# Third product read from PSUM in every three-term sum, blurred taps built on TensorE, and a new order at both ends of the program

## The chip, the cores and the metric

The kernel runs on one core of one Trainium2 chip. The metric is the device time of one launch in microseconds (us), as the median of several runs. Beside those runs stands one profiled execution, whose trace all the durations come from.

## The reference, cut to what matters

The input `x` is (128 samples, 64 channels, 1024 positions) in float32. Four modulated convolutions follow each other, and `x` is added to the result:

```python
TYPES = ('same', 'upsample', 'same', 'downsample')
def _layer(x, style, w, b, mw, mb, typ):
    s = style @ mw.T + mb                          # one factor per sample and input channel
    weight = SCALE * w * s[:, None, :, None]
    demod = lax.rsqrt(jnp.sum(weight * weight, axis=(2, 3)) + EPS)
    weight = weight * demod[:, :, None, None]      # one 64x64x3 filter per sample
    if typ == 'same':       out = conv_same(x, weight) + b
    elif typ == 'upsample': out = blur(conv_up(x, weight) + b, 2 * blur_k)
    else:                   out = conv_down(blur(x, blur_k), weight) + b
    return out
for i, typ in enumerate(TYPES):
    out = _layer(out, style, weights[i], biases[i], mod_w[i], mod_b[i], typ)
return x + out
```

All four layers are linear, so away from both ends of a row they are one filter of nine taps per sample (64x64 each), with the residual as an identity in the middle tap, and one constant per output channel. The three positions at each end of a row are computed separately, layer by layer.

## The kernel before, in words

**Tiling.** A pair `p` is two samples: 64 input channels of the one on the upper 64 partitions, those of the other on the lower 64. There are 64 pairs, and 32 steps `q` of two pairs each. Each matmul is 64x64 in one quadrant of the array, and four of them stand together. Everything is float32; the trace records two matmuls for each one that the program issues.

**The filter of a step.** For step `c` the nine taps are built from right to left. `scale3` (ScalarE, tiles `wd`) scales the last layer's weights; `stage1` multiplies them by layer 2's (PSUM tile `psS`, line 306) and ScalarE copies the result into `S` (line 284); `stage2` multiplies by `E` (`psR`, line 337), the seven blurred taps of layer 1, and ScalarE copies into `R`; `stage3` multiplies by layer 0's weights (`psW`, line 374, in two parts) and ScalarE copies into `Wf`. `E` is made once, at the start, by seven VectorE instructions in `blur` (line 275). `residual` adds the identity, and `combine` makes three weighted sums of the taps, `H` (lines 412 to 416, VectorE).

**The convolution of a pair.** Three output positions are computed with five products. `pre1` and `pre2` make five combinations `T` of the input's planes: VectorE makes `G` (lines 440 and 443), GpSimd (POOL) makes two of the `T` from it (447 and 448), VectorE the other three (453 and 463). `product(p, m, ...)` issues 12 matmuls for one of the five products. `convA12` issues products 1 and 2, and `convA3` product 3, into three column ranges of one PSUM tile `psA` (170 columns each; two such tiles turn, tag `u` of `ps_conv`). Products 0 and 4 are added by `convB` to the PSUM tile `Y`, which must already hold its start value. `seed` makes the start value and the middle output `y1` on VectorE: `u = -m2/3 - m1` and `v = m2/3 - m1` (lines 528 and 529), then `Y = u + m3 * (1/6, 4/6)` in one instruction for both column ranges (547) and `y1 = 2 * m3/6 + v` (548). For that, ScalarE first copies from `psA`: `-m1` (line 506, in `m1_copy`) and product 3 twice, times 1/6 and times 4/6 (519 and 520). All three copies are issued in `convA3`, behind product 3; for the last pair alone, `m1_copy` is issued in `convA12`. `output` scales `Y` and `y1` into the tile `o` (line 572, ScalarE), and `store` writes it out.

**Order.** The scheduler is off (`manual_schedule`): the order on each engine is that of the program's text, and semaphores are derived from the tiles that instructions share. One step of the main loop is: `stage2(c)`, `convB(p)`, `output(p)`, `stage3(c, 0)`, `convA12(p+2)`, `seed(p+1)`, `stage3(c, 1)`, `convA3(p+2)`, `convB(p+1)`, `output(p+1)` in both halves, `seed(p+2)`, `stage1(s)`, `scale3(s+1)`, `combine(c)`, `convA12(p+3)`, `convA3(p+3)`, with `c = q+2` and `s = q+3`. So the pairs with an even number have `stage3(c, 1)` between their products 2 and 3, and those with an odd number have nothing there. `EXTRA` and `SLOTS` put the remaining work on style factors, constants and row ends into fixed steps. `zeros_to_y` issues matmuls of zeros.

Of the kernel before, what the change touches and what calls it, by code (L numbers as in the profile page):

```python
# [50 lines left out]
NL = 4  # L53
C = 64
# [8 lines left out]
def kernel(  # L63
# [67 lines left out]
    eps = const.tile([P, 1], F32, name="eps")  # L131
    Z = const.tile([P, 512], F32, name="Z")
    E = const.tile([P, NT, C], F32, name="E")
    nc_v.memset(one, 1.0)
    nc_v.memset(Z, 0.0)
    nc_v.memset(E, 0.0)
    nc_v.memset(eps, EPS)
# [21 lines left out]
    def y_bank(p, s):  # L159
        return Y2[p][s] if p in Y2 else Y[:, s]  # L160
# [110 lines left out]

    def blur(i, j):
        for b in range(i, j):
            dst = E[:, b : b + K, :]
            nc_v.scalar_tensor_tensor(dst, w1r, BLUR2[b], dst, op0=ALU.mult, op1=ALU.add)

# [49 lines left out]
    def stage2(q, pool=None, engs=(nc_a, nc_a), between=None):  # L326
        st = chain[q]
        ps = unit(pool or ps_w, f"psR{q}")
        for n, e in enumerate((-2, -1, 0, 1, 2, 3, 4, 5, 6)):
            if e % 2 == 0:  # L330
                a, lo, m = slice(0, 5, 2), e // 2 + 1, 3
            else:
                a, lo, m = slice(1, 4, 2), (e + 3) // 2, 2
            for r, rows in enumerate(HALF):
                for c, cols in enumerate(HALF):
                    src = st[c if r == 0 else 1 - c]
                    nc.tensor.matmul(  # L337
                        ps[r][cols, lo * C : (lo + m) * C],
                        E[rows, e + 2, :],
                        src[rows, a, :],  # L340
                        start=(n == 0),
                        stop=(n == 8),
                        skip_group_check=True,
                    )
# [61 lines left out]
    def combine(q):  # L406
        W, H_ = Wq[q]
        chain.pop(q)
        a, b, c = (W[:, :, i::K, :] for i in range(K))
        h1, h2, h3 = (H_[:, i] for i in range(3))  # L410

        nc_v.scalar_tensor_tensor(h2, c, -0.5, a, op0=ALU.mult, op1=ALU.add)
        nc_v.tensor_add(h1, h2, b)  # L413
        nc_v.tensor_sub(h2, h2, b)
        nc_v.scalar_tensor_tensor(h3, c, -1.5, h2, op0=ALU.mult, op1=ALU.add)
        nc_v.scalar_tensor_tensor(h3, b, 3.0, h3, op0=ALU.mult, op1=ALU.add)

# [15 lines left out]
    def pre1(p, eng=nc_g):  # L433
# [12 lines left out]
        load(p + NX, slice(0, 1))  # L446
        eng.tensor_add(t[:, 2, :NJ], plane(g, 2), plane(g, 1))  # L447
        eng.tensor_sub(t[:, 3, :NJ], plane(g, 2), plane(g, 1))  # L448

# [43 lines left out]
    def convA12(p):  # L493
# [6 lines left out]
        part[p] = m  # L500
        if p == NP - 1:
            m1_copy(p)

    def m1_copy(p):
        m1s[p] = m_tile("m1", p)
        nc_a.activation(m1s[p], part[p][0], AF.Copy, scale=-1.0)  # L506

    m1s = {}

    def convA3(p):  # L510
        if p >= NP:
            return
        m = part[p]
        product(p, 3, [m[2][:, s] for s in range(2)])
        if p not in m1s:
            m1_copy(p)
        m1 = m1s.pop(p)
        m3 = m_tile("m3", p, (2, 2, NB))
        nc_a.activation(m3[:, :, 0, :], m[2], AF.Copy, scale=1.0 / 6.0)
        nc_a.activation(m3[:, :, 1, :], m[2], AF.Copy, scale=4.0 / 6.0)  # L520
        part[p] = (m1, m[1], m3)

    def seed1(p):
        if p >= NP:
            return
        m1, m2, m3 = part.pop(p)
        u, v = m_tile("u", p), m_tile("v", p)
        nc_v.scalar_tensor_tensor(u, m2, -1.0 / 3.0, m1, op0=ALU.mult, op1=ALU.add)  # L528
        nc_v.scalar_tensor_tensor(v, m2, 1.0 / 3.0, m1, op0=ALU.mult, op1=ALU.add)  # L529
        part[p] = m3, u, v  # L530

    y1s = {}

    def seed2(p):
        if p >= NP:
            return
        m3, u, v = part.pop(p)
        y1s[p] = y1 = m_tile("y1", p)
        uu = u[:, :, None, :].to_broadcast([P, 2, 2, NB])
        blocks = lambda y: y[..., : 2 * NB].rearrange("c s (i j) -> c s i j", i=2)  # L540
        if p in Y2:
            for s in range(2):
                nc_v.tensor_add(
                    blocks(y_bank(p, s)[:, None, :]), uu[:, s : s + 1], m3[:, s : s + 1]
                )
        else:
            nc_v.tensor_add(blocks(Y), uu, m3)  # L547
        nc_v.scalar_tensor_tensor(y1, m3[:, :, 0, :], 2.0, v, op0=ALU.mult, op1=ALU.add)  # L548

# [275 lines left out]
    nc_a.activation(wsq[T, :2], wio[T, :2], AF.Square)  # L825
    nc_v.tensor_mul(wsq[T, 2:], wio[T, 2:], wio[T, 2:])
    zeros_to_y(4, 256)
    mod_scale(PART[0], pm[0][0])
# [4 lines left out]
    var_matmul(PART[0], pm[0][1])  # L833
    blur(0, 1)
    var_root(PART[0], pm[0][1])
    mod_matmul(LATER, pm[1][0])

    zeros_to_y(4, 256)
    weight_sums()
    first_inverse(PART[0])  # L840
    table_A(PART[0], d2)
    scale3(0, BOTH)
    scale3(1)
    nc_a.copy(raw[0][:, 0, :n_later], pm[1][0][:, :n_later])
# [80 lines left out]
    def layers(i, j):  # L925
# [3 lines left out]
    EXTRA = {  # L929
        (0, 1): lambda: mod_scale(REST, raw[0][:, 0], LATER),  # L930
        (1, 0): lambda: (table_B(REST), vector_a1(REST)),
        (1, 1): lambda: (var_root(REST, after(0)), const_rest(0, PART[1], after(1))),
        (2, 0): lambda: (var_inverse(*layers(2, 3)), table_0(REST), vector_b1(REST)),
        (2, 1): lambda: (const_rest(1, PART[1], after(0)), var_newton(*layers(2, 3))),
        (3, 0): lambda: (table_A(REST, dm[:, 2, REST]), table_02(REST), vector_c2(REST)),
        (3, 1): lambda: (const_rest(2, PART[1], after(0)), var_inverse(*layers(1, 2))),
        (4, 0): lambda: (var_inverse(*layers(0, 1)), vector_Da(REST)),
        (4, 1): lambda: (var_newton(*layers(0, 2)), table_C(REST), vector_c0(REST)),
        (5, 0): lambda: var_inverse(*layers(3, 4)),
        (5, 1): lambda: (  # L940
            const_rest(0, REST, after(0)),
            var_newton(*layers(3, 4)),
            table_3(REST),
        ),
        (6, 0): lambda: setup_x(0),
        (6, 1): lambda: const_rest(1, REST, after(0)),
# [19 lines left out]
    for q in range(NQ):  # L966
# [28 lines left out]
        if q:  # L995
            pre2(p + 3)
            store(p, 0)
            pre1(p + 4)
            store(p, 1)
            seed(p + 1)  # L1000
        else:
            store(p, 0)
            seed2(p + 1)
            pre2(p + 3)
            store(p, 1)
            pre2b(p + 2)
            pre1(p + 4)
        EXTRA.get((q, 0), lambda: None)()
# [3 lines left out]
        if q == NQ - 2:  # L1012
            convA12(p + 3)
        side = SLOTS.get(q)
        convB(p + 1, (lambda: slot(*side)) if side else None)
        if q == NQ - 2:
            seed(p + 2)
        output(p + 1, 0)
        output(p + 1, 1, nc_a if q < NQ - 2 else nc_v)
        if c == NQ - 1:  # L1020
# [3 lines left out]
            zeros_to_y(2, 2 * NB, p + 2)  # L1024
        pre2(p + 4)
        store(p + 1, 0)
        pre1(p + 5)
        store(p + 1, 1)
        if q < NQ - 2:
# [78 lines left out]
```

## Time and profile before

| what | value |
|---|---|
| three timed runs, median (lowest to highest) | 517.96 us (516.3 to 518.59) |
| the profiled execution's own time | 515.94 us |
| its span, first to last instruction | 514.1 us |
| mean granted TensorE clock | 0.993 |
| TensorE matmuls busy | 492.9 us (96%) |
| VectorE busy | 476.7 us (93%) |
| ScalarE busy | 364.0 us (71%) |
| GpSimd busy | 159.7 us (31%) |

In the trace's lines PE is TensorE (PEld its weight loads), DVE VectorE, ACT ScalarE, POOL GpSimd. A group line has the source line, engine, operation, tiles as out<-in, shapes and count, then busy us and mean ns of one, then the engine's idle time just before and what ended it. A timeline line has start (us), duration (us), engine, line, operation, tiles, shapes and count, and in brackets the idle time before it where there was a wait. The mean of a pipelined matmul (some 300 ns) is a latency; what one costs is read from the distance between starts.

### The profile page before, as it was taken

What the parts mean: (1) busy time and instruction counts of PE and PEld (TensorE: products, weight loads), DVE (VectorE), ACT (ScalarE), POOL (GpSimd) and SP (SyncE); (2) the same over time, 40 slices, a digit from 0 to 9 for tenths busy, and PEclk for the clock granted to TensorE, in tenths of its full rate; (3) what the DMA queues carried; (4) which work ended last, traced back from release to release, by engine and by line L of the source; (5) the groups of instructions that cost most, each with busy time, mean ns of one, the idle gap of its engine ahead of it and who ended that gap; (6) DMA issues with size and microseconds to landing.
All of it is one profiled execution on the core that took longest, in us unless ns stands there. A gap on an engine that the chain in (4) does not pass through costs nothing.

```text
span 514.1 us, 28399 instructions
## 1 busy us (share of the span) xinstructions
PE 492.9 (96%) x12612; PEld 467.9 (91%) x12612; DVE 476.7 (93%) x869; ACT 364.0 (71%) x908; POOL 159.7 (31%) x196
## 2 busy tenths in 40 slices
PE   8998699998999999999999999999999999999994
PEld 5997699998899989999999999889999999999983
DVE  6899989999999999999989999989999979999994
ACT  3466567776766877777877777777777768777753
POOL 3315633443423331322221332331333213322210
PEclk9999999999999999999999999999999999999998
DMA  7125544553434544544554454554555435543223
GB/s 253 44 70 159 162 128 126 167 152 103 145 117 155 166 133 125 159 131 126 166 155 128 136 140 122 160 154 129 138 164 153 149 118 173 154 137 126 84 86 123
DMA packets 37162, 70.91 MB, mean 138 GB/s; under 512 B 4144, under 2 KB 28464, under 8 KB 37040
## 3 DMA queue, kind: packets, MB, share of 16 engines
q1 hardware_dynamic: 36960, 68.85, 44.3%
q8 instruction: 99, 1.62, 1.4%
q10 hardware_dynamic: 80, 0.25, 0.1%
q14 instruction: 23, 0.19, 0.1%
HBM read 35.46 MB, written 33.62 MB: 134 GB/s over the span
## 4 chain that ended last, share of the span: by engine, by line
PE 65%; DVE 20%; ACT 3%; issue 2%; DVEq 0%
PE psA L481 21%; PE Y L481 18%; PE psR L337 11%; PE psW L374 9%; PE psS L306 4%; DVE Y L547 3%; DVE T L463 3%; DVE y L548 2%; DVE G L440 2%; PE psE L724 2%; ACT o L572 2%; DVE G L443 1%; DVE u L528 1%; DVE T L453 1%; DVE H L413 1%
## 5 line engine op out<-in xcount | busy, mean ns | idle before, releaser
L481 PE MATMUL psA<-T,H 64*64 64x170 f32 x4608 | 193.9, 304 | 1.0 <-DVE v L529 1.0
L481 PEld LDWEIGHTS psA<-T,H 64*64 64x64 f32 x4608 | 176.9, 133 | 2.2 <-issue 1.6
L447 POOL TENSOR_TENSOR T<-G 128x342 f32<-128x342 f32 x62 | 57.0, 920 | 312.8 <-DVE G L443 266.7
L481 PE MATMUL Y<-T,Wf 64*64 64x170 f32 x3072 | 131.3, 307 | 12.0 <-DVE Y L547 10.9
L481 PEld LDWEIGHTS Y<-T,Wf 64*64 64x64 f32 x3072 | 115.9, 133 | 18.0 <-DVE Y L547 15.0
L572 ACT ACTIVATE o<-Y,oc,dm 128x340 f32<-128x340 f32 (+1 forms) x126 | 79.8, 633 | 48.0 <-PE Y L481 47.2
L374 PE MATMUL psW<-R,par_oi 64*64 64x256 f32 (+3 forms) x1536 | 92.4, 350 | 0.0
L284 ACT ACTIVATE Wf<-psW,t 128x256 f32<-128x256 f32 (+1 forms) x252 | 75.3, 381 | 22.5 <-PE psW L374 22.2
L337 PE MATMUL psR<-S,E 64*64 64x192 f32 (+1 forms) x2304 | 89.7, 299 | 0.2 <-ACT S L284 0.2
L547 DVE TENSOR_TENSOR Y<-u,m 128x680 f32<-128x680 f32 x62 | 67.2, 1083 | 17.2 <-ACT o L572 17.0
L337 PEld LDWEIGHTS psR<-S,E 64*64 64x64 f32 x2304 | 81.6, 133 | 1.7 <-ACT S L284 0.7
L448 POOL TENSOR_TENSOR T<-G 128x342 f32<-128x342 f32 x62 | 82.0, 1323 | 0.0
L374 PEld LDWEIGHTS psW<-R,par_oi 64*64 64x64 f32 x1536 | 73.2, 133 | 8.0 <-PE Y L643 0.3
L572 ACT ACTIVATE o<-y,oc,dm 128x170 f32<-128x170 f32 x125 | 65.8, 526 | 0.3 <-DVE y L548 0.3
L284 ACT ACTIVATE R<-psR,tC 128x448 f32<-128x448 f32 x63 | 36.5, 630 | 40.5 <-PE psR L337 40.5
L548 DVE SCALAR_TENSOR_TENSOR y<-m,v 128x340 f32<-128x340 f32 x64 | 60.2, 940 | 0.0
L440 DVE SCALAR_TENSOR_TENSOR G<-X 128x688 f32<-128x688 f32 x64 | 56.4, 882 | 0.0
L463 DVE TENSOR_TENSOR T<-G 128x684 f32<-128x684 f32 x64 | 56.3, 881 | 0.0
L306 PE MATMUL psS<-wd,par_oi 64*64 64x192 f32 x768 | 40.3, 324 | 0.0
L506 ACT ACTIVATE m<-psA 128x340 f32<-128x340 f32 x64 | 29.3, 458 | 10.4 <-PE psA L481 7.6
L306 PEld LDWEIGHTS psS<-wd,par_oi 64*64 64x64 f32 x768 | 32.2, 133 | 1.4 <-ACT wd L284 0.5
L528 DVE SCALAR_TENSOR_TENSOR u<-psA,m 128x340 f32<-128x340 f32 x64 | 32.1, 502 | 0.8 <-ACT m L520 0.8
(127 smaller groups left out, 446.1 us busy)
## 6 DMA issues: line engine op xcount, KB each, us to landing
out<-o SPq DMA_DIRECT2D x128, 255.0 KB, 3.6
X<-in_x SPq DMA_DIRECT2D x60, 344.0 KB, 3.2
X<-in_x SPq DMA_DIRECT2D x60, 172.0 KB, 3.5
X<-in_x SPq DMA_DIRECT2D x4, 516.0 KB, 6.5
Xe<-in_x_ends SPq DMA_DIRECT2D x1, 512.0 KB, 4.0
par_oi<-in_params_oi SPq DMA_DIRECT2D x2, 208.0 KB, 4.9
par_io<-in_params_io ACTq DMA_DIRECT2D x1, 240.0 KB, 3.8
par_io<-in_params_io SPq DMA_DIRECT2D x1, 240.0 KB, 4.4
```

Source lines behind the costliest of these rows:

```text
L284: nc_a.activation(dst, src, AF.Copy, scale=f)
L306: nc.tensor.matmul(ps[r][cols, k * C : (k + K) * C], woi[rows, 2, k, :], src[rows, :], start=(k == 0), stop=(k == K - 1), skip_group_check ...
L337: nc.tensor.matmul(ps[r][cols, lo * C : (lo + m) * C], E[rows, e + 2, :], src[rows, a, :], start=(n == 0), stop=(n == 8), skip_group_check ...
L374: nc.tensor.matmul(ps[r][cols, (lo - t_lo) * C : (hi - t_lo) * C], woi[rows, 0, k, :], rt[c][rows, lo - k : hi - k, :], start=(k == order[0]),
L440: nc_v.scalar_tensor_tensor(g[:, PL:], X[:, : 2 * PL], 0.5, X[:, PL:], op0=ALU.mult, op1=ALU.subtract)
L447: eng.tensor_add(t[:, 2, :NJ], plane(g, 2), plane(g, 1))
L448: eng.tensor_sub(t[:, 3, :NJ], plane(g, 2), plane(g, 1))
L463: nc_v.tensor_sub(t[:, 0:2, :NJ], both(a, PL), both(b, 1))
L481: nc.tensor.matmul(ps[s][cols], w, Ts[p][rows, SLOT[m], j : j + NB], start=(g == 0 and m not in (0, 4)), stop=(g == 2), skip_group_check=True,
L547: nc_v.tensor_add(blocks(Y), uu, m3)
L548: nc_v.scalar_tensor_tensor(y1, m3[:, :, 0, :], 2.0, v, op0=ALU.mult, op1=ALU.add)
L572: nc_a.activation(dst, src, AF.Identity, bias=add, scale=d3)
```

## The change

1. **Sums.** `seed` no longer uses copies of product 3. `y1`, and the two column ranges of `Y` (one instruction each now), read product 3 from PSUM. The two copies on ScalarE (lines 519 and 520) are gone.
2. **`m1_copy`** is issued in `convA12`, behind product 2 and ahead of product 3, for every pair.
3. **Blur.** ScalarE scales layer 1's taps by the four different blur factors (`w1s`); 28 matmuls with an identity add them up in `Y`; one ScalarE and one VectorE copy move them to `E`, whose taps are stored in another order (even ones first).
4. **`combine`** has another order, `residual` within it, and 2.0 where 3.0 stood.
5. **The start** has another order: `mod_matmul(LATER)` behind `stage1(0)`, `pre1(0)` and the first part of `pre1(1)` earlier, `pre2b` a step earlier, fewer zero matmuls; in step 0 `pre1(4)` and `pre1(5)` run wholly on VectorE, and stores and `pre1` change places.
6. **`EXTRA` and `SLOTS`** for the last 96 samples' style factors begin one step later.
7. **The end:** in step 30 `convA3(63)` and `seed1(63)` stand ahead of `convB(61)`, and `pre2(63)` behind `seed(61)`; in step 31 only `seed2(63)` is left.

The core of the diff:

```diff
+    def blur_scale():
+        for i in range(K + 1):
+            nc_a.activation(w1s[:, i], w1r, AF.Copy, scale=BLUR2[i])
+    def blur_matmul(ps):
+        for b in range(len(BLUR2)):
+            w = w1s[:, min(b, len(BLUR2) - 1 - b)]
+            for r, rows in enumerate(HALF):
+                both = b % 2 == r
+                src = w[rows, 0::2] if both else w[rows, 1]
+                at = (b if both else b + 1) // 2
+                for cols in HALF:
+                    nc.tensor.matmul(ps[r][cols, C * at : C * (at + 1 + both)], idn[rows], src, ...)
...
         nc_v.scalar_tensor_tensor(h2, c, -0.5, a, op0=ALU.mult, op1=ALU.add)
+        residual(q)
+        nc_v.scalar_tensor_tensor(h3, c, -1.5, h2, op0=ALU.mult, op1=ALU.add)
         nc_v.tensor_add(h1, h2, b)
         nc_v.tensor_sub(h2, h2, b)
-        nc_v.scalar_tensor_tensor(h3, c, -1.5, h2, op0=ALU.mult, op1=ALU.add)
-        nc_v.scalar_tensor_tensor(h3, b, 3.0, h3, op0=ALU.mult, op1=ALU.add)
+        nc_v.scalar_tensor_tensor(h3, b, 2.0, h3, op0=ALU.mult, op1=ALU.add)
...
         product(p, 1, [m[0][:, s] for s in range(2)])
         product(p, 2, [m[1][:, s] for s in range(2)])
         part[p] = m
-        if p == NP - 1:
-            m1_copy(p)
+        m1_copy(p)
...
     def convA3(p):
-        if p >= NP:
-            return
-        m = part[p]
-        product(p, 3, [m[2][:, s] for s in range(2)])
-        if p not in m1s:
-            m1_copy(p)
-        m1 = m1s.pop(p)
-        m3 = m_tile("m3", p, (2, 2, NB))
-        nc_a.activation(m3[:, :, 0, :], m[2], AF.Copy, scale=1.0 / 6.0)
-        nc_a.activation(m3[:, :, 1, :], m[2], AF.Copy, scale=4.0 / 6.0)
-        part[p] = (m1, m[1], m3)
+        if p < NP:
+            m3 = part[p][2]
+            product(p, 3, [m3[:, s] for s in range(2)])
+    def sum_of(out, x, f, y):
+        nc_v.scalar_tensor_tensor(out, x, f, y, op0=ALU.mult, op1=ALU.add)
...
+        sum_of(u, m2, -1.0 / 3.0, m1)
+        sum_of(v, m2, 1.0 / 3.0, m1)
+        sum_of(y1s[p], m3, 2.0 / 6.0, v)
...
+        for i, f in enumerate((1.0 / 6.0, 4.0 / 6.0)):
+            for k, y in banks:
+                sum_of(y[..., i * NB : (i + 1) * NB], m3[:, k], f, u[:, k])
```

In the built program, the first matmul of product 3 of every pair waits for the semaphore of this pair's `m1_copy`, and that copy waits for the last matmul of product 2. Before, only the last pair had this wait.

More of the change, by code (lines that the diff above doesn't have):

```diff
@@ L133 @@
     E = const.tile([P, NT, C], F32, name="E")
+    w1s = const.tile([P, K + 1, K, C], F32, name="w1s")
     nc_v.memset(one, 1.0)
     nc_v.memset(Z, 0.0)
-    nc_v.memset(E, 0.0)
     nc_v.memset(eps, EPS)
@@ L269, in table_3, with blur_copy @@
         table(nc_g, t3, bs, ALT, ODD, dm[:, 3, bs], var[:, 3, bs])
[L272 to L275, printed above, removed]
+    def blur_scale():
[9 more added lines that the diff above has]
+                for cols in HALF:
+                    nc.tensor.matmul(
+                        ps[r][cols, C * at : C * (at + 1 + both)],
+                        idn[rows],
+                        src,
+                        start=(b == 0),
+                        stop=(b == len(BLUR2) - 1),
+                        skip_group_check=True,
+                    )
+    def blur_copy(ps, engs):
+        for r, (i, j) in enumerate(((0, 5), (5, NT))):
+            dst, src = E[:, i:j].rearrange("c e i -> c (e i)"), ps[r][:, : (j - i) * C]
+            if engs[r] is nc_a:
+                nc_a.copy(dst, src)
+            else:
+                engs[r].tensor_copy(dst, src)
     w3 = wio[:, 3]
@@ L338, in stage2 @@
                         ps[r][cols, lo * C : (lo + m) * C],
[L339 removed]
+                        E[rows, e // 2 + 1 + (e % 2) * 5, :],
                         src[rows, a, :],
@@ L446, in pre1, with rest @@
         load(p + NX, slice(0, 1))
-        eng.tensor_add(t[:, 2, :NJ], plane(g, 2), plane(g, 1))
-        eng.tensor_sub(t[:, 3, :NJ], plane(g, 2), plane(g, 1))
+        def rest(eng):
+            eng.tensor_add(t[:, 2, :NJ], plane(g, 2), plane(g, 1))
+            eng.tensor_sub(t[:, 3, :NJ], plane(g, 2), plane(g, 1))
+        if eng is None:
+            return rest
+        rest(eng)
     def pre2a(p, eng=nc_v):
@@ L500, in convA12 @@
         part[p] = m
-        if p == NP - 1:
-            m1_copy(p)
+        m1_copy(p)
     def m1_copy(p):
-        m1s[p] = m_tile("m1", p)
-        nc_a.activation(m1s[p], part[p][0], AF.Copy, scale=-1.0)
-    m1s = {}
+        m = part[p]
+        m1 = m_tile("m1", p)
+        nc_a.activation(m1, m[0], AF.Copy, scale=-1.0)
+        part[p] = (m1, *m[1:])
     def convA3(p):
-        if p >= NP:
-            return
-        m = part[p]
-        product(p, 3, [m[2][:, s] for s in range(2)])
-        if p not in m1s:
-            m1_copy(p)
-        m1 = m1s.pop(p)
-        m3 = m_tile("m3", p, (2, 2, NB))
-        nc_a.activation(m3[:, :, 0, :], m[2], AF.Copy, scale=1.0 / 6.0)
-        nc_a.activation(m3[:, :, 1, :], m[2], AF.Copy, scale=4.0 / 6.0)
-        part[p] = (m1, m[1], m3)
+        if p < NP:
+            m3 = part[p][2]
+            product(p, 3, [m3[:, s] for s in range(2)])
+    y1s = {}
+    def sum_of(out, x, f, y):
+        nc_v.scalar_tensor_tensor(out, x, f, y, op0=ALU.mult, op1=ALU.add)
     def seed1(p):
@@ L527, in seed1 @@
         u, v = m_tile("u", p), m_tile("v", p)
[L528 to L532, printed above, removed]
+        y1s[p] = mpool.tile([P, 2, NB], F32, tag="y1", name=f"y1_{p}", bufs=3)
+        sum_of(u, m2, -1.0 / 3.0, m1)
+        sum_of(v, m2, 1.0 / 3.0, m1)
+        sum_of(y1s[p], m3, 2.0 / 6.0, v)
+        part[p] = m3, u
     def seed2(p):
@@ L536, in seed2 @@
             return
[L537 to L548, printed above, removed]
+        m3, u = part.pop(p)
+        banks = [(slice(s, s + 1), y_bank(p, s)[:, None]) for s in range(2)]
+        if p not in Y2:
+            banks = [(slice(0, 2), Y)]
+        for i, f in enumerate((1.0 / 6.0, 4.0 / 6.0)):
+            for k, y in banks:
+                sum_of(y[..., i * NB : (i + 1) * NB], m3[:, k], f, u[:, k])
     def seed(p):
@@ L826 @@
     nc_v.tensor_mul(wsq[T, 2:], wio[T, 2:], wio[T, 2:])
+    blur_scale()
     zeros_to_y(4, 256)
@@ L833 @@
     var_matmul(PART[0], pm[0][1])
-    blur(0, 1)
     var_root(PART[0], pm[0][1])
-    mod_matmul(LATER, pm[1][0])
-    zeros_to_y(4, 256)
+    psB = [Y[:, r] for r in range(2)]
+    blur_matmul(psB)
     weight_sums()
@@ L842 @@
     scale3(0, BOTH)
-    scale3(1)
-    nc_a.copy(raw[0][:, 0, :n_later], pm[1][0][:, :n_later])
-    blur(1, 3)
+    blur_copy(psB, BOTH)
     var_inverse(PART[0])
@@ L850 @@
     stage1(0, None, BOTH)
+    mod_matmul(LATER, pm[1][0])
+    scale3(1)
+    nc_a.copy(raw[0][:, 0, :n_later], pm[1][0][:, :n_later])
     scale3(2)
-    zeros_to_y(2, 256)
-    blur(3, 7)
+    pre1(0, nc_v)
     mod_scale(PART[1], raw[0][:, 0], LATER)
@@ L857 @@
     stage2(0, None, BOTH)
-    pre1(0, nc_v)
     pre2a(0)
@@ L862 @@
     const_rest(0, PART[0], const_of(0, PART[0]))
+    rest_of_1 = pre1(1, None)
     stage3(0, 0, None, BOTH)
@@ L869 @@
     pre2b(0)
+    rest_of_1(nc_v)
     stage3(0, 1, None, BOTH)
@@ L872 @@
     const_first(2, PART[0])
-    residual(0)
     combine(0)
+    const_rest(2, PART[0], const_of(2, PART[0]))
     stage2(1, ps_conv)
@@ L877 @@
     convA3(0)
-    pre1(1, nc_v)
     pre2a(1)
+    pre1(2)
     stage3(1, 0)
@@ L882 @@
     seed(0)
-    pre1(2)
+    pre2b(1)
     convA12(1)
@@ L886 @@
     convA3(1)
-    const_rest(2, PART[0], const_of(2, PART[0]))
-    residual(1)
     combine(1)
     pre2a(2)
+    pre1(3)
     seed1(1)
-    pre2b(1)
-    pre1(3)
+    pre2b(2)
     var_inverse(PART[1])
@@ L905, in var_and_constant @@
         var_matmul(REST, ps[0])
-        const_matmul(0, PART[1], ps[1])
+        const_matmul(1, PART[1], ps[1])
     SLOTS = {
-        1: (var_and_constant, NL * n, n1),
-        2: (lambda ps: const_matmul(1, PART[1], ps[0]), n1),
+        1: (lambda ps: const_matmul(0, PART[1], ps[0]), n1),
+        2: (var_and_constant, NL * n, n1),
         3: (lambda ps: const_matmul(2, PART[1], ps[0]), n1),
@@ L929 @@
     EXTRA = {
[L930 to L943, printed above, removed]
-        ),
-        (6, 0): lambda: setup_x(0),
+        (1, 1): lambda: (
+            mod_scale(REST, raw[0][:, 0], LATER),
+            const_rest(0, PART[1], after(0)),
+        ),
+        (2, 0): lambda: (table_B(REST), vector_a1(REST)),
+        (2, 1): lambda: (var_root(REST, after(0)), const_rest(1, PART[1], after(1))),
+        (3, 0): lambda: (var_inverse(*layers(2, 3)), table_0(REST), vector_b1(REST)),
+        (3, 1): lambda: (const_rest(2, PART[1], after(0)), var_newton(*layers(2, 3))),
+        (4, 0): lambda: (
+            table_A(REST, dm[:, 2, REST]),
+            var_inverse(*layers(1, 2)),
+            table_02(REST),
+            vector_c2(REST),
+        ),
+        (4, 1): lambda: (var_inverse(*layers(0, 1)), vector_Da(REST)),
+        (5, 0): lambda: (var_newton(*layers(0, 2)), table_C(REST), vector_c0(REST)),
+        (5, 1): lambda: (const_rest(0, REST, after(0)), var_inverse(*layers(3, 4))),
+        (6, 0): lambda: (var_newton(*layers(3, 4)), table_3(REST), setup_x(0)),
         (6, 1): lambda: const_rest(1, REST, after(0)),
@@ L979 @@
         if q == NQ - 1:
-            seed(p + 1)
+            seed2(p + 1)
         output(p, 1, nc_a if q < NQ - 1 else nc_v)
@@ L995 @@
         if q:
-            pre2(p + 3)
+            if q < NQ - 2:
+                pre2(p + 3)
             store(p, 0)
@@ L1000 @@
             seed(p + 1)
+            if q == NQ - 2:
+                pre2(p + 3)
         else:
             store(p, 0)
+            store(p, 1)
             seed2(p + 1)
             pre2(p + 3)
-            store(p, 1)
-            pre2b(p + 2)
-            pre1(p + 4)
+            pre1(p + 4, nc_v)
         EXTRA.get((q, 0), lambda: None)()
@@ L1013 @@
             convA12(p + 3)
+            convA3(p + 3)
         side = SLOTS.get(q)
@@ L1017 @@
             seed(p + 2)
+            seed1(p + 3)
         output(p + 1, 0)
@@ L1024 @@
             zeros_to_y(2, 2 * NB, p + 2)
[L1025 to L1028, printed above, removed]
+        if q:
+            pre2(p + 4)
+            store(p + 1, 0)
+            pre1(p + 5)
+            store(p + 1, 1)
         if q < NQ - 2:
@@ L1035 @@
         if c < NQ:
-            residual(c)
-            combine(c)
+                combine(c)
+        if q == 0:
+            store(p + 1, 0)
+            store(p + 1, 1)
+            pre2(p + 4)
+            pre1(p + 5, nc_v)
         EXTRA.get((q, 1), lambda: None)()
@@ L1040 @@
             convA12(p + 3)
-        convA3(p + 3)
+            convA3(p + 3)
 def kernel(x, cond_512, L0_cond_weights, L0_cond_biases, L0_cond_mod_w, L0_cond_mod_b):
```

## The prediction

> **What bounds the kernel now.** I read the busy shares first, then the waits of the tensor engine, then the stretches in which it waits, and last one step in order of time. The page:
>
> ```profile
> PE 492.9 (96%) x12612; PEld 467.9 (91%) x12612; DVE 476.7 (93%) x869; ACT 364.0 (71%) x908; POOL 159.7 (31%) x196
> ...
> L547 DVE TENSOR_TENSOR Y<-u,m 128x680 f32<-128x680 f32 x62 | 67.2, 1083 | 17.2 <-ACT o L572 17.0
> ...
> L548 DVE SCALAR_TENSOR_TENSOR y<-m,v 128x340 f32<-128x340 f32 x64 | 60.2, 940 | 0.0
> ...
> L528 DVE SCALAR_TENSOR_TENSOR u<-psA,m 128x340 f32<-128x340 f32 x64 | 32.1, 502 | 0.8 <-ACT m L520 0.8
> ```
>
> TensorE and VectorE are both nearly full. A busy TensorE need not be at its peak, so I checked starts: a group of four 64x64 matmuls with 170 columns begins 144 ns after the one before it in almost all of the trace, so TensorE works at its own rate there. One product (three groups, two records for each matmul) is 0.86 us. Seen also: the sum with two SBUF operands (548) takes 940 ns, the one with a PSUM operand and the same 340 elements (528) takes 502. The timeline shows why: 548 takes 1.22 us when GpSimd's 448 runs beside it and 0.50 when not; 528 stays at 0.50 in both cases.
>
> Where TensorE does wait, the view of busy time by stretch and the list of waits tell:
>
> ```profile
> 31.00:72.00 41.00, 34.66 (x860) 32.58 (x855) 39.03 (x68) 25.31 (x66) 19.73 (x36) 0.96 0.46 135
> 72.00:200.00 128.00, 124.82 (x3248) 120.07 (x3244) 124.88 (x231) 94.84 (x240) 44.59 (x45) 1.00 0.47 138
> ```
> ```profile
> PEld Y L481 <- DVE Y L547: 15.0, 14, 3.1
> ```
>
> The columns of the first view are window, length, then PE, PEld, DVE, ACT, POOL busy, the clock, DMA. Between 31 and 72 us VectorE is busy for 39.0 of 41 us and TensorE stands still three times before `Y` (2.5, 1.6 and 3.0 us longer than its own work); behind the third, from 63.0 to 66.5 us, the granted clock is 0.51. From 72 to 350 us eleven smaller gaps at the same place add up to 7.6 us. At the end two more make 2.3 us. All the rest of the span is TensorE's own work, the start (about 13 us ahead of its steady rate) and 6.1 us behind the last matmul. So at most some 17 us can be had by a lighter VectorE; whatever makes TensorE wait in each step is paid in full.
>
> The step that the change touches most, in order of time (second half of a step, an odd pair):
>
> ```profile
> 81.39 0.63 ACT L572 ACTIVATE o<-Y,oc,dm 128x340 f32<-128x340 f32 x1 [0.52 <-PE Y L481]
> ...
> 81.92 0.52 ACT L572 ACTIVATE o<-y,oc,dm 128x170 f32<-128x170 f32 x1
> 82.07 2.82 PE L481 MATMUL psA<-T,H 64*64 64x170 f32 x72
> ...
> 82.34 0.63 ACT L572 ACTIVATE o<-Y,oc,dm 128x340 f32<-128x340 f32 x1
> ...
> 82.86 0.52 ACT L572 ACTIVATE o<-y,oc,dm 128x170 f32<-128x170 f32 x1
> ...
> 83.28 0.93 ACT L284 ACTIVATE S<-psS,tB 128x320 f32<-128x320 f32 x2
> ...
> 84.10 0.80 ACT L284 ACTIVATE wd<-par_io,tA 128x192 f32<-128x192 f32 x2
> ...
> 84.66 1.64 PE L337 MATMUL psR<-S,E 64*64 64x192 f32 x40
> ...
> 85.02 0.45 ACT L506 ACTIVATE m<-psA 128x340 f32<-128x340 f32 x1
> ```
>
> The reader is to see that TensorE runs the three products without a break (72 records, 82.07 to 84.66) and goes on with `psR`, while ScalarE is still at the four outputs, two `S` and two `wd` that stand ahead of the copy. The copy starts only at 85.02, and today no matmul waits for it.
>
> **The change, part by part.** *The early copy* (the step that decides). In the built program product 3 waits for the `-m1` copy of its own pair. For an odd pair nothing lies between products 2 and 3, so TensorE stops until ScalarE has worked off its queue. From the lines above: product 3 would begin at 82.07 + 2 x 0.863 = 83.80. ScalarE is free of `wd` at about 84.8, with the copy starting between 84.8 and 85.0; I take 84.9. It takes 0.45, and a matmul starts 0.05 behind what it waits for (547 ended at 62.36, its matmul began at 62.41): 85.40. The stop is 1.6 us; the same sum in the step at 45 us gives 1.47, over all odd pairs the middle is 1.56. I take 1.55. Everything behind it on TensorE (`stage2`, the next `convB`) moves by as much, since this queue is in order and has no slack. Odd pairs of steps 0 to 27: 28 x 1.55 = 43.4. Step 2 has a square root of 0.61 (line 207) ahead of the copy: 0.6. Step 28 has no `wd`: 0.8. Step 29 has neither `S` nor `wd`, but zero matmuls in between: 0.25. Pairs 62, 63 and 0 have nothing in between: 0.8 each, 2.4. For the 30 even pairs from pair 2 on, `stage3(c, 1)` (0.98 us) lies in between; the copy would end 0.07 us after that work, so the stop is about 0.12: 3.6. Sum 51.1 us. The bound from below is the round trip with a free ScalarE: latency of the last matmul 0.30, 0.11 to the copy (psA ended at 84.89 above, the copy began 0.13 later), 0.45, 0.05, less the 0.1 to the next start: 0.8 per odd pair. From above 1.75, if each copy starts 0.2 later.
>
> [...]
>
> *The sums.* Per pair VectorE spends 1083 + 940 ns now; three sums with a PSUM operand take 3 x 502: 0.52 less, 1.03 us per step. VectorE is busy for 124.9 of 128 us, with 14.5 us from step to step 14.2 per step; so 13.1 remain. That ends the waits before `Y`: -7.6. No row reads and writes PSUM in one VectorE instruction; the nearest are 528 (0.50) and 547 (1.08, it writes PSUM). I take 0.50, by 528, since 547 without GpSimd beside it takes 0.86 for twice the elements, as 463 does into SBUF (0.86). With the longer step VectorE only becomes the bound if a `Y` sum takes over 0.50 + (16.2 - 13.1)/4 = 1.3 us. The ScalarE copies that go (458 + 470 ns a pair) stand behind the early copy, so their going shortens no wait. `psA` is now held until the last `Y` sum; that sum stands ahead of `convB` of its pair and the tile is wanted only behind that, so no wait is added but at the end.
>
> [...]
>
> *Steps 0 and 1.* `blur` leaves VectorE (2.7 us), four adds of `pre1(4)` and `pre1(5)` come to it (4 x 0.43). I walked VectorE's new order by start-to-start distances: before `convB(1)` a stop of 1.3 stays of 2.5, before `convB(2)` nothing of 1.6, before `convB(3)`, where TensorE now comes later, 0.9 of 3.0. That is -4.9; and without a stop of 3 us no half clock follows: -1.3 (1.0 in the `Y` matmuls, the rest in the variance matmuls). Together -6.2, with bounds 0 and -8.4.
>
> *The start.* The blur matmuls (2688 columns over four quadrants, 0.6 us at the steady rate) lie behind 7.48 us, when the last weights land, and ahead of 9.9, when `stage1(0)` begins; the scaling on ScalarE (four of 0.46) ends before the square root at 7.50. Cost nothing; without that cover 0.6. `psR` of step 0 no longer waits for `E`: -0.4. But `pre1(1)`'s adds (2 x 0.43) and `residual` (2 x 0.39) now come ahead of `h1`, which `product(0, 1)` needs and which today is there 0.7 us ahead: +1.2. Together +0.8, bounds -0.4 and +2.
>
> *The end.* Of two waits (0.99 for `v`, 1.3 for `Y`) the first goes and 0.4 of the second stays: -1.9, bounds 0 and -2.3.
>
> Moved loads, stores, `EXTRA` and `SLOTS`: SP's queue has the same 128 stores and 124 loads, and a store or load is waited for by nothing on TensorE's path (none is in the list of waits behind 10 us); 0, bounds +-0.5.
>
> **Sum.** 51.1 - 7.6 - 6.2 + 0.8 - 1.9 = +36.2 us on the profiled execution: span 550.3, its time 515.9 + 36.2 = 552.1. The median of the runs shown is 2.0 above that execution, so 554.1 by them; I forecast between both, **553 us**.
>
> **Rivals.** (1) *The copy is always done in time* or the wait isn't there in effect, and the change does what it says: -7.6 - 4.6 (the stop before `convB(3)` then keeps 2.5) + 0.8 - 1.4, some 505 us. For it: TensorE's only long waits today are for VectorE. Against: ScalarE's queue in the lines above. (2) *The bare round trip* of 0.8 per odd pair: about 27 in place of 51.1, some 529. For it: ScalarE is busy only 71%. Against: all of its outputs fall just there. (3) *VectorE becomes the bound*, because sums from PSUM into PSUM take more than 1.3 us: at 1.5 each, 4 x 0.2 x 31 = 25 more, some 578. Nothing in the trace speaks for it but that no row shows it.
>
> **Chances.** Forecast 0.84, (1) 0.07, (2) 0.06, (3) 0.03. Range: the early copy's stop of 1.35 to 1.75 per odd pair alone is -6 to +6, the bounds of the other parts widen it by some 5 either way: 541 to 564. I leave out (1), (2) and (3), 0.16 in all. Half a per cent is about what a measurement of this kernel can tell from no change, and no case ends within it; faster comes from (1) alone: faster 0.07, same 0.01, slower 0.92.
>
> **What would show it.** Right: TensorE (psA) waiting for ScalarE (m) over thirty times, 1.2 to 1.5 us each and 40 us or more in all; no TensorE wait for `Y` behind 72 us; `y1` at 0.50 us always; line 448 of GpSimd at 0.92 in place of 1.32; 16.2 us from step to step. Wrong: `psA` with 72 records in 2.6 us as now, a copy that starts less than 0.3 us after product 2, or a `Y` sum over 0.6 us.

## The result and the profile after

| | before | after |
|---|---|---|
| median (lowest to highest) of 4 runs | 517.96 us (516.3 to 518.59) | **553.52 us** (553.17 to 553.77) |
| ratio, 95% interval | | 1.0691 [1.0666, 1.0717] |
| profiled execution: its time, span | 515.94, 514.1 us | 553.39, 551.6 us |
| mean granted clock | 0.993 | 0.999 |

The changed kernel is 7% slower, and the forecast of 553 us held. The page of after, its busy shares and the groups that answer to those shown of before (the sums are all at line 552 now, product 3 at line 516):

```profile
PE 499.9 (91%) x12644; PEld 454.9 (82%) x12644; DVE 439.1 (80%) x932; ACT 318.2 (58%) x785; POOL 127.6 (23%) x192
...
L516 PE MATMUL psA<-T,H 64*64 64x170 f32 x4608 | 194.2, 307 | 39.1 <-ACT m L541 38.2
...
L479 POOL TENSOR_TENSOR T<-G 128x342 f32<-128x342 f32 x60 | 55.2, 920 | 0.0
...
L552 DVE SCALAR_TENSOR_TENSOR y<-psA,v 128x340 f32<-128x340 f32 x64 | 32.7, 511 | 2.2
L552 DVE SCALAR_TENSOR_TENSOR u<-psA,m 128x340 f32<-128x340 f32 x64 | 32.2, 504 | 2.6 <-PE psA L516 2.6
```

Every engine but TensorE has less to do than before: VectorE 439 us in place of 477, ScalarE 318 in place of 364. The sum `y` fell from 940 to 511 ns, and GpSimd's second sum (479, formerly 448) from 1323 to 920. None of that shows in the time, because of the second line: TensorE stands idle for 39.1 us ahead of `psA`, 38.2 of them for ScalarE's copy `m`. The list of waits of after says the same (engine and what waits, releaser, us in total, times, longest):

```profile
PEld psA L516 <- ACT m L541: 53.0, 62, 2.1
...
PE psA L516 <- ACT m L541: 38.2, 33, 1.8
...
PEld psE L656 <- POOL c0f L642: 2.2, 1, 2.2
```

The wait of weight loads (PEld) for `m` comes 62 times. Ahead of `Y`, where the kernel before waited 15.0 us for VectorE, 1.9 are left. The busy times by stretch, same windows and columns as for before:

```profile
31.00:72.00 41.00, 37.20 (x965) 34.31 (x958) 38.38 (x81) 23.56 (x61) 8.85 (x26) 1.00 0.42 133
72.00:200.00 128.00, 116.69 (x3004) 107.20 (x2995) 104.45 (x227) 78.25 (x197) 35.47 (x48) 1.00 0.43 130
```

Up to 72 us after is ahead (TensorE 37.2 us busy against 34.7, no fall of the clock). Behind it TensorE has lost 11.3 of 128 us, and VectorE, which was full before, is idle for 23.5. One odd pair of a step in the middle, in order of time (start, duration, engine, line, operation):

```profile
329.58 0.52 ACT L598 ACTIVATE o<-y,oc,dm 128x170 f32<-128x170 f32 x1
...
329.77 1.92 PE L516 MATMUL psA<-T,H 64*64 64x170 f32 x48
...
330.94 0.94 ACT L312 ACTIVATE S<-psS,tB 128x320 f32<-128x320 f32 x2
331.76 0.80 ACT L312 ACTIVATE wd<-par_io,tA 128x192 f32<-128x192 f32 x2
...
332.45 0.45 ACT L541 ACTIVATE m<-psA 128x340 f32<-128x340 f32 x1
...
332.95 1.10 PE L516 MATMUL psA<-T,H 64*64 64x170 f32 x24 [1.27 <-ACT m L541]
```

Where the kernel before had 72 records without a break, there are now 48, a stop, and 24. Products 1 and 2 are TensorE's own work until 329.77 + 2 x 0.863 = 331.50; product 3 begins at 332.95. The stop is 1.5 us. (The 1.27 in brackets counts from the modelled end of the last matmul; distances between starts don't depend on that model, and are what is used below.) The copy could have started at about 331.8, when product 2 was through, but ScalarE was at `S` and `wd` until 332.5.

### The profile page after: what moved, and what is told of

Read it like the earlier page. It is cut to its first block, busy times and chain, and to the rows that moved or that the text cites. A ratio compares the mean times of both kernels' runs of the same rounds, so it can differ in the third digit from the quotient of the medians.

```text
span 551.6 us, 28423 instructions
## 1 busy us (share of the span) xinstructions
PE 499.9 (91%) x12644; PEld 454.9 (82%) x12644; DVE 439.1 (80%) x932; ACT 318.2 (58%) x785; POOL 127.6 (23%) x192
## 5 line engine op out<-in xcount | busy, mean ns | idle before, releaser
L516 PE MATMUL psA<-T,H 64*64 64x170 f32 x4608 | 194.2, 307 | 39.1 <-ACT m L541 38.2
L516 PEld LDWEIGHTS psA<-T,H 64*64 64x64 f32 x4608 | 164.2, 133 | 55.2 <-ACT m L541 53.0
L478 POOL TENSOR_TENSOR T<-G 128x342 f32<-128x342 f32 x60 | 55.0, 917 | 381.3 <-PE Y L516 203.5
L552 DVE SCALAR_TENSOR_TENSOR Y<-psA,u 128x340 f32<-128x340 f32 (+1 forms) x132 | 66.5, 508 | 87.7 <-ACT o L598 85.5
L516 PE MATMUL Y<-T,Wf 64*64 64x170 f32 x3072 | 124.7, 304 | 2.3 <-DVE Y L552 2.3
L402 PE MATMUL psW<-R,par_oi 64*64 64x256 f32 (+3 forms) x1536 | 85.3, 349 | 0.0
L312 ACT ACTIVATE Wf<-psW,t 128x256 f32<-128x256 f32 (+1 forms) x252 | 75.5, 382 | 15.8 <-PE psW L402 15.8
L365 PEld LDWEIGHTS psR<-S,E 64*64 64x64 f32 x2304 | 77.2, 133 | 2.9 <-ACT Wf L312 0.5
L402 PEld LDWEIGHTS psW<-R,par_oi 64*64 64x64 f32 x1536 | 60.6, 133 | 14.4
L479 POOL TENSOR_TENSOR T<-G 128x342 f32<-128x342 f32 x60 | 55.2, 920 | 0.0
L552 DVE SCALAR_TENSOR_TENSOR y<-psA,v 128x340 f32<-128x340 f32 x64 | 32.7, 511 | 2.2
L472 DVE SCALAR_TENSOR_TENSOR G<-X 128x342 f32<-128x342 f32 x64 | 32.6, 510 | 0.0
L488 DVE TENSOR_TENSOR T<-X 128x342 f32<-128x342 f32 x64 | 32.4, 506 | 0.1
```

What stands on the lines that cost most here:

```text
L312: nc_a.activation(dst, src, AF.Copy, scale=f)
L365: nc.tensor.matmul(ps[r][cols, lo * C : (lo + m) * C], E[rows, e // 2 + 1 + (e % 2) * 5, :], src[rows, a, :], start=(n == 0), stop=(n == 8 ...
L402: nc.tensor.matmul(ps[r][cols, (lo - t_lo) * C : (hi - t_lo) * C], woi[rows, 0, k, :], rt[c][rows, lo - k : hi - k, :], start=(k == order[0]),
L472: nc_v.scalar_tensor_tensor(plane(g, 2), plane(X, 3), 0.5, plane(X, 2), op0=ALU.mult, op1=ALU.subtract)
L516: nc.tensor.matmul(ps[s][cols], w, Ts[p][rows, SLOT[m], j : j + NB], start=(g == 0 and m not in (0, 4)), stop=(g == 2), skip_group_check=True,
L552: nc_v.scalar_tensor_tensor(out, x, f, y, op0=ALU.mult, op1=ALU.add)
```

## The experiments

"Stop" is the time from the first start of a group of matmuls to the first start of the next one, less TensorE's own rate for that group; the 0.05 us that the first four matmuls behind a stop lose are counted in (in after the next four start 195 ns behind them, where it is 144 ns elsewhere). The theory is the prediction's: product 3 waits for its own pair's copy, and the copy for ScalarE's queue. Unless said otherwise a kernel is the changed one with the edit shown.

**The copy behind product 3 (`e1_late_copy`).** One line moved back:

```diff
     def convA12(p):
         part[p] = m
-        m1_copy(p)
     def convA3(p):
             product(p, 3, [m3[:, s] for s in range(2)])
+            m1_copy(p)
```

> The changed kernel with the copy of -m1 issued behind product 3 again, all else kept. Theory (product 3 waits for a copy that stands at the end of ScalarE's queue): the stops of TensorE in front of product 3, 28 x 1.51 and some 8 us more by the trace after, all go, and the time falls from 553.5 to 501 to 508 us, with no wait of psA for ScalarE left. Rival 1 (product 3 read from PSUM by VectorE slows TensorE or holds psA): the time stays above 540. Rival 2 (the new order at both ends costs the time): it stays above 540 too, with the loss before 60 us and behind 530 us.

Measured: **505.49 us** (504.38 to 507.12), ratio to before 0.9767 [0.9731, 0.9802]. The same changed kernel without the early copy is 48.0 us faster. Its page:

```profile
PE 488.4 (97%) x12644; PEld 476.8 (95%) x12644; DVE 439.4 (87%) x932; ACT 322.3 (64%) x785; POOL 128.2 (25%) x192
```

No wait of TensorE for `m` at `psA` is left in it. Both rivals of the expectation fall: neither the sums nor the orders cost time, the place of one copy does. It also answers the prediction's first rival: its 505 us was the right price for "no stop".

**The early copy alone (`e2_before_early_copy`).** The kernel before, with

```diff
-        if p == NP - 1:
-            m1_copy(p)
+        m1_copy(p)
```

> The kernel before with one edit: the copy of -m1 ahead of product 3 for all pairs. Theory: the stop comes without the rest of the change, about 1.5 us for each odd pair; the later steps absorb the 7.6 us of waits for Y and part of those in steps 0 and 1, so 518 + 51 - 12 = 557, between 550 and 563 us. Rivals 1 and 2: nothing of theirs is in it, so 518.

Measured: **553.45 us** (553.2 to 556.03), ratio 1.0696 [1.0663, 1.073]. This one line costs as much as the whole change, and its steps repeat 16.05 us apart as after's do. All that the rest of the change saves is nothing once TensorE stops in each step. (Its page and steps are of the execution of 556.03 us, in which the granted clock was at 0.50 from 63.8 to 70.7 us.) A detail of the page shows why the terms don't add up in this kernel:

```profile
L448 POOL TENSOR_TENSOR T<-G 128x342 f32<-128x342 f32 x62 | 66.0, 1064 | 0.0
...
L547 DVE SCALAR_TENSOR_TENSOR y<-m,v 128x340 f32<-128x340 f32 x64 | 41.5, 649 | 0.0
```

The old sum with two SBUF operands, 940 ns in the kernel before, averages 649 here: in the longer step 13 of the 64 sums run beside GpSimd's 447 or 448 (1214 ns each), where it was 39 before (1220 ns each); the others take 504 to 505 ns in both.

**The scaling behind the copy (`e3_scale_behind`).** The early copy stays; the two `wd` that stood ahead of it in ScalarE's queue are issued after it:

```diff
-        if s + 1 < NQ:
-            scale3(s + 1)
         ...
             convA12(p + 3)
+            if s + 1 < NQ:
+                scale3(s + 1)
             convA3(p + 3)
```

> The changed kernel with the two scaled copies wd of an odd step's end issued behind the copy of -m1 in ScalarE's queue. Theory (what stands ahead of the copy in the queue sets the stop): each stop of steps 0 to 27 shrinks by the two wd, 0.72 us, 20 us in all: 533 us, with 0.8 us a stop left. Rival (the stop is a bare round trip between two engines, whatever the queue): 553, unchanged.

Measured: **536.96 us** (536.13 to 537.27), ratio 1.0364 [1.034, 1.0389]: 16.6 us less than after, where 20 was expected. First ScalarE, then TensorE in its timeline:

```profile
337.06 0.94 ACT L312 ACTIVATE S<-psS,tB 128x320 f32<-128x320 f32 x2
337.94 0.45 ACT L541 ACTIVATE m<-psA 128x340 f32<-128x340 f32 x1
338.29 0.79 ACT L312 ACTIVATE wd<-par_io,tA 128x192 f32<-128x192 f32 x2
```
```profile
335.90 1.92 PE L516 MATMUL psA<-T,H 64*64 64x170 f32 x48
338.44 1.10 PE L516 MATMUL psA<-T,H 64*64 64x170 f32 x24 [0.63 <-ACT m L541]
```

The copy now starts at 337.94, 0.31 us behind the end of TensorE's own work on product 2 (335.90 + 1.73 = 337.63). The stop is 338.44 - 337.63 = 0.81, with the 0.05 behind it 0.87. In step 29 of after, where neither `S` nor `wd` stands ahead of the copy, ScalarE was idle and waited for product 2:

```profile
526.71 1.91 PE L516 MATMUL psA<-T,H 64*64 64x170 f32 x48
528.75 0.46 ACT L541 ACTIVATE m<-psA 128x340 f32<-128x340 f32 x1 [0.36 <-PE psA L516]
529.25 1.10 PE L516 MATMUL psA<-T,H 64*64 64x170 f32 x24 [0.63 <-ACT m L541]
```

There too the copy starts 0.31 behind product 2 (526.71 + 1.73 = 528.44), and the stop is the same. So 0.87 is the bare round trip TensorE to ScalarE and back, and the other 0.64 of after's 1.51 was ScalarE's queue. Of the 28 odd pairs of steps 0 to 27, 18 come down to 0.87; the others keep up to 1.15, and step 2 1.38. Over all 28 the stops fell by 17.0 us, of which 16.6 came out. The queue theory holds in kind; the 20 that was expected took 0.72 for the queue.

**Other work between products 2 and 3 (`e5_stage1_between`).** The early copy stays, and `stage1(s)` with its ScalarE work stands between the two products:

```diff
-        if s < NQ:
-            stage1(s)
-        if s + 1 < NQ:
-            scale3(s + 1)
         ...
             convA12(p + 3)
+        if s < NQ:
+            stage1(s)
+        if s + 1 < NQ:
+            scale3(s + 1)
             convA3(p + 3)
```

> The early copy stays, but the first blur stage and the scaling of its weights are issued between products 2 and 3 of the odd pairs, so that 0.98 us of other matmuls run while the copy is made. Theory (a bare round trip TensorE-ScalarE-TensorE of 0.87 us, as the run with the scaling moved showed it, and ScalarE's queue for the rest of the 1.51 us): the stop in front of product 3 goes, but the two S copies (0.94 us and their hand-over) are now only 0.86 us ahead of the stage that reads them, a stop of about 0.5 us; 553.5 - 28 x 1.5 + 28 x 0.5 gives 525 us, 518 to 530. Rival (a guarded product 3 costs its stop wherever it stands): 550 to 554. Rival (the S copies take the whole place of the m1 copy): 537 or more.

Measured: **521.99 us** (521.71 to 522.28), ratio 1.0071 [1.0053, 1.0089]. The wait is still there in the program, but TensorE does not stand at it, as the timeline of the odd pair shows:

```profile
325.25 1.91 PE L516 MATMUL psA<-T,H 64*64 64x170 f32 x48
326.98 1.16 PE L334 MATMUL psS<-wd,par_oi 64*64 64x192 f32 x24
327.39 0.44 ACT L541 ACTIVATE m<-psA 128x340 f32<-128x340 f32 x1
327.95 1.05 PE L516 MATMUL psA<-T,H 64*64 64x170 f32 x24
```

326.98 and 327.95 lie 0.97 apart, `psS`'s own work, and the copy ran in that time (327.39 to 327.83). The second rival's full price falls with it; the stop that the theory put at `stage2` is 0.3 us in place of 0.5. Covered by 0.97 us of other matmuls, the guarded product has no stop of its own. It remains 16.5 us over the late copy, and the trace shows 0.54 a step: 0.33 within `psR`, where the second `S` is just late, and 0.2 at the even pair's `psW`.

**The sums alone (`e4_sums_alone`).** The kernel before with after's `seed1` and `seed2` (three-operand sums that read `m3` from `psA`), copy behind product 3, no other part of the change.

> The kernel before with the new sums alone: product 3 read from PSUM, its two copies gone, the copy of -m1 behind product 3; blur, order at both ends and combine as before. Theory: VectorE's relief ends the waits for Y behind 72 us (7.6) and most of those of steps 0 and 1 (4 to 6): 504 to 508 us. Rival 1: slower than 518. Rival 2: as the theory here, and faster than the changed kernel with the late copy.

Measured: **507.57 us** (506.44 to 509.96), ratio 0.9805 [0.977, 0.9841]. The sums without any new order save 10.6 us.

**The orders alone (`e8_old_sums`).** The reverse: after's orders and blur, before's sums with their two copies, copy behind product 3.

> The changed kernel's orders, TensorE's blurred taps and the copy behind product 3, but the sums as before (two scaled copies of product 3 by ScalarE, sums of two SBUF operands). Theory (the sums and the orders add up: 10.6 us for the sums alone, 12.7 for both): 516 us, ratio to before 0.996. Rival (the orders need the lighter VectorE to pay or the other way around): 509 to 512 if they pay most where VectorE is full, 518 or more if they pay nothing there.

Measured: **509.72 us** (509.47 to 510.63), ratio 0.9837 [0.9818, 0.9856]. The additive theory, 516, fails. Sums alone save 10.6 us, orders alone 8.1 (517.78 - 509.72), both 12.7: they stand in for each other. The likely reason, by the stops below, is that both shorten the same waits ahead of `Y`, of which there were 17 us or so. In this kernel the old sum still takes 851 ns and VectorE is 90% busy, yet between 72 us and the end its stops for a sum ahead of `Y` are only 0.41, 0.33 and 1.02 (one of 0.86 at 312.5 us, within `Y`'s matmuls, waited for nothing that the profile shows). Its largest stop, 3.75 us in step 5, is of another kind (`c0f`, see the next run; 2.24 in `e1_late_copy`). Which of the reordered pieces spares it the stops ahead of `Y` was not separated.

**The missed stop (`e6_constant_earlier`).** On `e1_late_copy`, the making of `c0f` for the last 96 samples half a step earlier, as before had it:

```diff
-        (4, 1): lambda: (var_inverse(*layers(0, 1)), vector_Da(REST)),
-        (5, 0): lambda: (var_newton(*layers(0, 2)), table_C(REST), vector_c0(REST)),
+        (4, 1): lambda: (var_inverse(*layers(0, 1)), vector_Da(REST),
+            var_newton(*layers(0, 2)), table_C(REST), vector_c0(REST)),
```

> The kernel with the copy behind product 3, and c0f of the last 32 batches made half a step earlier (as in the kernel before), ahead of its matmul in step 5. Theory (the move of this work by half a step, which the prediction priced at nothing, cost a stop of 2.0 us there): 503.4 us, 505.5 less 2.0 to 2.2, ratio to before 0.972. Rival (GpSimd is late with c0f in both places, or TensorE catches up behind it): 505.5 us, ratio 0.976.

Measured: 505.52 us (503.26 to 506.61), ratio 0.9745 [0.9717, 0.9772]: by the medians, nothing. The trace shows that the stop itself went (2.24 us before the constant's matmul), with 1.07 left before `Y` just ahead of it, some 1.2 gained, and that this execution lost 1.7 us at another place. The stretch around TensorE's pause for `Y` in step 1, in this kernel (the clock is the first figure behind the POOL column):

```profile
57.00:60.50 3.50, 1.24 (x40) 0.95 (x33) 3.43 (x8) 1.48 (x5) 1.77 (x2) 1.00 1.00 381
60.50:64.00 3.50, 3.50 (x66) 3.50 (x70) 3.47 (x7) 0.75 (x3) 0.54 (x1) 0.65 0.47 148
```

and in `e1_late_copy`:

```profile
57.00:60.50 3.50, 1.23 (x40) 0.94 (x33) 3.43 (x8) 1.49 (x5) 1.78 (x2) 1.00 1.01 374
60.50:64.00 3.50, 3.50 (x96) 3.50 (x100) 3.47 (x7) 1.56 (x4) 1.13 (x2) 1.00 0.50 151
```

The same pause of 2.3 us; behind it the clock stays whole in the one execution and falls to 0.65 in the other, with 66 matmuls for 96 in the same time. Of the five executions of `e6_constant_earlier`, the two with a mean clock of 0.998 and 0.999 took 503.3 and 503.6 us, the three with 0.994 and 0.995 took 505.5 to 506.6. So the theory's 503.4 is met in the two executions with the higher mean clock, and the rival's 505.5 by the medians, though not for the rival's reason.

**The sums ahead of the inputs (`e7_start_order`).** As `e6_constant_earlier`, with `seed(2)` ahead of `pre2` and `pre1` in step 1, and `h1` before `h3` in `combine`.

> As the run with c0f earlier, and in step 1 the sums of pair 2 ahead of VectorE's work on the next inputs, and h1 made one instruction before h3. Theory (TensorE's stop of 2.3 us at 58 us is VectorE's late seed of Y and nothing else, and each pair of inputs has slack): 503.4 less 2.0 to 2.6, about 501 us, ratio to before 0.967. Rival (the inputs' work behind the sums becomes late in its turn, the stop moves to the next products): 503 to 505 us.

Measured: 506.23 us (504.43 to 506.52), ratio 0.9756 [0.9734, 0.9778]. The rival holds in kind: the stop at 57 us went, and TensorE stopped for 2.6 us at 73 us, again for VectorE's sum ahead of `Y`, with a lower clock behind it:

```profile
75.50:79.50 4.00, 4.00 (x68) 4.00 (x72) 3.97 (x7) 0.55 (x2) 1.42 (x3) 0.61 0.47 144
```

The time is above both forecasts. In this run VectorE's backlog was handed on, not removed.

**Less work for VectorE there (`e9_gpsimd_start`).** As `e6_constant_earlier`, the two sums per pair of inputs in step 0 by GpSimd:

```diff
-            pre1(p + 4, nc_v)
+            pre1(p + 4)
...
-            pre1(p + 5, nc_v)
+            pre1(p + 5)
```

> As the run with c0f earlier (copy behind product 3), and in step 0 the two sums per pair of inputs by GpSimd instead of VectorE, which gives VectorE 4 x 0.5 us back before 57 us, where GpSimd stands idle from 45.3 to 58 us. Theory (VectorE is full from 43 to 60 us, TensorE's pause of 2.3 us at 58 us is its backlog, and the dip of the granted clock behind the pause, in those executions that have one, goes with it): pause under 0.5 us, granted clock 0.998 or 0.999 in all executions, 501.5 us (503.3 to 503.6 in the executions without the dip, less 2.0), ratio to before 0.968. Rival (as in the run that put the sums first: the pause only moves to the next products, as it is made of more than this work, and the clock falls there in some executions): 503 to 506 us.

Measured: **501.74 us** (501.61 to 502.32), ratio 0.971 [0.9687, 0.9733], the fastest of all. Its first window:

```profile
57.00:60.50 3.50, 3.18 (x91) 2.90 (x87) 3.46 (x7) 1.78 (x7) 3.50 (x16) 1.00 0.94 330
```

TensorE is busy for 3.18 us in place of 1.24, the stop is 0.54, and the five executions lie within 0.7 us of each other. The time is as the theory had it (501.5); the clock is not quite, 0.996 to 0.999 where 0.998 or 0.999 was expected of all.

## Why the prediction was right

By its own steps, each against the trace of after:

| step | predicted us | measured us |
|---|---|---|
| odd pairs of steps 0 to 27 | 28 x 1.55 + 0.6 = 44.0 | 27 x 1.52 + 2.06 = 43.1 |
| steps 28 and 29 | 0.8 and 0.25 | 0.87 and 0.87 |
| pairs 62, 63 and 0 | 2.4 | 1.78 + 0.85 = 2.6 |
| 30 even pairs | 30 x 0.12 = 3.6 | 30 x 0.10 = 3.0 |
| **early copy in all** | **51.1** | **50.5** |
| waits before `Y` behind 72 us | -7.6 | -7.6 (none over 0.3 left) |
| steps 0 and 1, with the clock | -6.2 | -6.6 |
| start | +0.8 | +1.65 |
| end | -1.9 | -1.6 |
| `EXTRA` and `SLOTS` | 0 (+-0.5) | +2.0 |
| span | +36.2 | +37.5 |

The measured parts add up to 38.3; the other -0.8 is spread over small waits and was not traced. Of the signs that the prediction named, the waits of `psA` for `m` came 33 times with 38.2 us in all, the step is 16.05 us, and `y` takes 0.51 us and GpSimd's second sum 0.92 throughout; behind 72 us TensorE waits for a sum ahead of `Y` once, at the very end.

- *The early copy.* The wait, its queue and its price came out of the lines of before: ScalarE's free time read there, the round trip added. `e1_late_copy` shows the price as a whole (48.0 us, against 50.5 by stops), `e2_before_early_copy` that it needs no other part of the change. The bound from below, 0.8 for a bare round trip, is the 0.87 of `e3_scale_behind` and of steps 28 and 29. Step 29 was sized wrong: the zero matmuls lie ahead of product 1 (their 0.57 stood in the trace of before too), not between products 2 and 3, so the full 0.87 is paid.
- *The sums.* 0.50 us was taken for a sum from PSUM into PSUM that no row showed. The group of `Y` in after, 124 sums of that kind with 128x340 elements, has a mean of 519 ns. The third rival needed over 1.3. The gain is real (`e4_sums_alone`: 10.6 us) and lies in VectorE's time, for which the changed kernel has no use.
- *Steps 0 and 1.* The three stops of before (7.1 us in all) became 0.87, none and 0.86, where 1.3, none and 0.9 were expected; no half clock followed (1.00 from 31 to 72 us in after).
- *The start.* `pre1(1)` and `residual` ahead of `h1` do stop TensorE: 1.17 us ahead of product 1, as the +1.2 had it. Where TensorE stands in all is read from the first matmul of pair 2, in the kernel before and in after:

```profile
37.15 0.45 PE L481 MATMUL psA<-T,H 64*64 64x170 f32 x3
39.65 0.45 PE L516 MATMUL psA<-T,H 64*64 64x170 f32 x3
```

That is 2.50 us later, 0.85 of it the stop of pair 0, so 1.65. Of these, 0.60 stands already at the first matmul that waits for an input (`psM`, at 3.73 us before and at 4.33 in after). In the seven runs built on after it starts anywhere from 3.53 to 4.29, so this part is the input's arrival in these two executions, not the change. The blur's matmuls were mis-sized: they are 56 records and 1.14 us at the steady rate, where 0.6 counted each matmul once. They still cost nothing, since `stage1(0)` begins 0.60 later (10.51 for 9.91), as `psM` did.
- *The end.* From the first matmul of pair 60 to the start of the last matmul after takes 24.52 us in place of 23.41, with 2.75 of early copies in it: -1.6. The first of the two stops went, but the second hardly shrank (1.35 before, 1.28 in after), where 0.4 was expected:

```profile
506.04 1.96 PE L481 MATMUL Y<-T,Wf 64*64 64x170 f32 x48 [1.09 <-ACT o L572]
```
```profile
543.55 1.96 PE L516 MATMUL Y<-T,Wf 64*64 64x170 f32 x48 [1.04 <-DVE Y L552]
```
- *What was missed* is the last part, "Moved loads, stores, `EXTRA` and `SLOTS`", priced at 0. The prediction looked at the queues of loads and stores, not at who reads what `EXTRA` makes. In step 5 the constant's matmul stands between products 0 and 4, so its operand `c0f` is on TensorE's path, and its makers had moved from (4, 1) to (5, 0) while the matmul stayed in step 5:

```profile
127.47 1.41 POOL L251 TENSOR_TENSOR tC<-dm 64x48 f32<-64x48 f32 x2 [3.43 <-DVE dm L221]
128.96 0.86 POOL L642 TENSOR_TENSOR c0f<-dm,par_s 128x96 f32<-128x96 f32 x1
```

GpSimd's timeline of after: it waits for VectorE's `dm` until 127.47 and ends `c0f` at 129.82, while TensorE wanted it 2.0 us earlier. (In the kernel before, `c0f` was begun at 122.04 and its matmul at 126.03.) The step had room for this kind of work; one operation of it had a reader with a fixed place.

That the total came out within 1 us is luck in part: more than half of the unforeseen 2.0 of `c0f` and of what start and end cost beyond their terms is made up for by small misses the other way and by waits that the prediction didn't count, and the forecast was put between the profiled execution and the median of the runs. The mechanism and the size of the early copy are not luck: they were read from the lines of before, and `e1_late_copy` and `e2_before_early_copy` show them alone.

## What to carry to other kernels

Before a copy is moved ahead of a matmul that writes the same PSUM tile, look at what the queue of the copying engine holds at that point, and whether the matmul engine has other work to do meanwhile: here an odd pair's wait cost 0.64 us of queue and a round trip of 0.87, in every step, and no stop of product 3 where 0.97 us of other matmuls lay in between (`e5_stage1_between`). The relieved VectorE gained time here only where TensorE waited for it, and two ways to relieve it did not add up (10.6 and 8.1 us alone, 12.7 together); in `e7_start_order` a new stop of 2.6 us at 73 us took the place of the one at 57. When side work is moved by half a step, follow each result to its reader, not only the queues that it passes.

## What the runs showed of the hardware that was not expected

- **The round trip.** TensorE's last matmul of product 2, a ScalarE copy of 128x340 from PSUM (0.45 us) and the next matmul cost a stop of 0.87 us with ScalarE free (step 29 of after); only half of that is the copy.
- **The clock after a pause is not the same each time.** A pause of 2.3 us (2.5 by the distance between starts) left the granted clock at 1.00 in the trace of `e1_late_copy` and at 0.65 in the next stretch of that of `e6_constant_earlier`, kernels with the same orders up to that point. In the kernel before it was 0.51 from 63.0 to 66.5 us, behind the stop of 3.0 us, and 1.00 behind those of 2.5 and 1.6; in `e7_start_order` it was 0.61 from 75.5 to 79.5 us, behind the stop of 2.6. With after's stops of 1.5 us, one in each step, the mean was 0.999. What decides between the two outcomes was not shown.
- **Two SBUF operands beside GpSimd.** In the kernel before, where `y` takes both operands from SBUF, 39 of its 64 sums ran beside GpSimd's second sum (448): these took 1220 ns, and 448 took 1541; the other 25 took 504. Of the 23 of 448 that ran without `y`, 21 took 907 to 926 ns and two 1186 and 1539. In after, with product 3 in PSUM, no `y` took over 514 ns, though 32 of the 64 ran beside GpSimd's second sum (479), and none of 479 took over 941. That the old sum's mean fell to 649 ns in `e2_before_early_copy`, where only the step grew longer, was not foreseen.
